# Attention, last two head pairs: values of both pairs in one PSUM bank, row sums in another, and exponentials of two key tiles added before they are summed

## The chip, the cores and the metric

The kernel runs on one core of a Trainium2 chip. The metric is the device time of one execution in microseconds (us). A core has five engines that each work through their own queue in order and wait for one another by semaphores: TensorE (PE in the profile; its weight loads are listed apart as PEld), VectorE (DVE), ScalarE (ACT), GpSimd (POOL) and SyncE (SP), which only issues DMAs here. TensorE writes its results into PSUM, which this kernel divides into eight banks of 128 partitions by 512 float32.

## The reference, cut to what matters

```python
x  = hidden_states                          # (1, 2048, 512), float32
xn = layernorm(x)
qkv = xn @ w_qkv.T                          # 16 heads of 32
scores = where(causal, (q @ k.T) / sqrt(32), lowest)
attn = softmax(scores) @ v                  # per head, 2048 x 2048 scores
out = x + attn @ w_o.T + ffn(xn)            # ffn: gated GELU, 512 -> 4096 -> 512, 4-bit weights
```

Softmax is computed as exp(score - row maximum), summed over the keys for each query ("row sums"), and the values' product is divided by that sum at the end.

## The kernel before, in words

Sixteen heads are handled as eight pairs (`NP = 8`). Queries go in four blocks of 512 columns (`qb` 0 to 3), keys in sixteen tiles of 128 (`kt`). Scores are made transposed: keys on the partitions, 512 queries along the columns. A *step* `n` is one key tile for one query block, `steps[n] = (qb, kt)`; there are 40 steps per pair. In a block, the last four key tiles (`kt >= 4 * qb`) are *diagonal*: only columns from `c0 = (kt - 4 * qb) * 128` on are computed, so their widths are 512, 384, 256 and 128. The other steps are *off-diagonal* and 512 wide. Block 0 has no off-diagonal steps, block 1 has 4, block 2 has 8 and block 3 has 12.

Pairs 0 to 5 run one at a time, each together with the search for the row maxima of a later pair. Their row sums are already taken from exponentials that GpSimd adds up over two steps (`add_up`, line 395) and that TensorE then sums with a matrix of ones (`add_rows`, line 354).

The last two pairs (6 and 7), for which no maxima remain to be found, run *together* in a loop over `together`, a list of the 40 steps in an order written out by hand: blocks in the order 1, 0, 2, 3, and in a block each diagonal step followed by a quarter of the off-diagonal ones. Nothing is rescheduled: the order in which the code calls the operations is the order of each engine's queue. One pass of this loop issues:

1. `score_cols` (line 280) and `add_scores` (line 295): for each of the four heads one small bf16 matmul that puts minus the row maximum into a PSUM bank, and one float32 matmul that adds the scores. Pair 6 uses the pool `ps_t`, pair 7 the pool `ps_s`, each of three banks, so a step's two banks of a pool are free again only when exponentials of the step before have been read out of them.
2. `attend` for the step before, called for pair 6 and then for pair 7: `add_values` (line 343), two matmuls of values with the exponentials of two heads, and `add_rows` (line 354), two of ones with the same exponentials. A pair's values lie in partitions 0 to 63 of one bank and its row sums in partitions 64 to 127 of the same bank (`m0` for pair 6, `m1` for pair 7).
3. The exponentials, pair 6 head 0, head 1, then pair 7 head 0, head 1. Off-diagonal steps only need ScalarE (line 309). A diagonal step first has VectorE limit the diagonal 128 columns to at most 0 in PSUM (line 643, "the limit"), then ScalarE's exponential (line 646), then GpSimd sets the keys that come after the query to 0 (`omit_later_keys`, line 324). They are written to `prob` tiles of [128, 2, 512], one for a pair and a step, from a pool of five.
4. What is left over: at a block's end `keep_attention` copies the two banks out (lines 422 and 423), `normalize_attention` then inverts the row sums in four parts on VectorE (line 444) and multiplies on GpSimd (line 446); and eight times `token_rest` prepares the tokens for the feed-forward part (line 656 on VectorE, "the mask"; line 659 on GpSimd; line 661 on VectorE in a later pass).

After the loop come the output projection (`po`, line 889, 64 matmuls), which TensorE begins with block 1, and the feed-forward part (lines 934 to 1009), which fills the rest of the span.

Of the kernel before, what the change touches and what calls it, by code (L numbers as in the profile page):

```python
# [38 lines left out]
F32 = mybir.dt.float32  # L39
F32R = mybir.dt.float32r  # L40
I32 = mybir.dt.int32
AF = mybir.ActivationFunctionType
ALU = mybir.AluOpType
# [3 lines left out]
P = 128  # L47
# [3 lines left out]
D = H // HEADS  # L51
NT = S // P
TB = 512
NTB = S // TB
NK = H // P
NOG = H // P
NP = HEADS // 2
# [17 lines left out]
STEPS = NTB * (NTB + 1) * 2  # L75
# [3 lines left out]
def block_kernel(  # L79
# [10 lines left out]
    nc = tc.nc  # L90
# [4 lines left out]
    def turn_tile(i, name, dtype=F32, shape=(P, TB)):  # L95
# [6 lines left out]
    aT = [  # L102
        [late.tile([P, TB], F32, tag=f"aT{og}_{b}", name=f"aT{og}_{b}") for b in range(NTB)]
        for og in range(NOG)
    ]
# [8 lines left out]
    with (  # L114
# [23 lines left out]
        ones = const.tile([P, D], F32, tag="ones", name="ones")  # L138
# [3 lines left out]
        v = [vals.tile([P, 4, H], F32, tag=f"v{b}", name=f"v{b}") for b in range(NTB)]  # L142
# [42 lines left out]
        units, steps, first = [], [], {}  # L185
# [80 lines left out]
        def rows_when_due():  # L266
            if due and tick[0] >= due[0][0]:
                rows_from_parts()
            tick[0] += 1
# [33 lines left out]
        def exponentials(p, n, tiles):  # L303
            qb, kt = steps[n]
            c0 = max(0, kt - 4 * qb) * P
            prob = probs.tile([P, 2, TB], F32, tag="prob", name=f"prob{p}_{n}")
            if kt < 4 * qb:
                for h, ps in enumerate(tiles):
                    nc.scalar.activation(prob[:, h, :], ps, AF.Exp)  # L309
                return prob  # L310


            clip = turn_tile(12 + n % 2, f"clip{p}_{n}", shape=(P, 2, P))
            for h, ps in enumerate(tiles):
                nc.scalar.activation(clip[:, h], ps[:, c0 : c0 + P], AF.Relu, scale=-1.0)
                if c0 + P < TB:
                    nc.scalar.activation(prob[:, h, c0 + P :], ps[:, c0 + P :], AF.Exp)
            diag = prob[:, :, c0 : c0 + P]
            nc.scalar.activation(diag, clip, AF.Exp, scale=-1.0)
            omit_later_keys(diag)  # L320
            return prob

        def omit_later_keys(diag):
            nc.gpsimd.affine_select(
                out=diag,
                in_=diag,
                compare_op=ALU.is_ge,
                fill=0.0,
                base=0,
                pattern=[[0, 2], [1, P]],  # L330
                channel_multiplier=-1,
            )

        avs, rows, sums = {}, {}, {}
# [64 lines left out]
        def attend(p, n, prob, first, last):  # L399

            qb, kt = steps[n]
            if first:
                avs[p, qb] = ps_m.tile([P, TB], F32, tag=f"m{p % 2}", name=f"av{p}_{qb}")
                rows[p, qb] = avs[p, qb]
            add_values(p, n, prob, 0, first, last)
            c0 = max(0, kt - 4 * qb) * P
            add_rows(p, qb, [prob[:, h] for h in range(2)], first, last, c0)
            if last:
                full.append((p, qb))

        full, invert = [], []

        def keep_attention():

            p, qb = full.pop(0)
            av, row = avs[p, qb], rows[p, qb]
            og, half = p // 2, slice(64 * (p % 2), 64 * (p % 2 + 1))
            if p % 2 == 0:
                sums[og, qb] = sump.tile([P, TB], F32, tag="sums", name=f"sums{og}_{qb}")
            if p >= NP - 2:  # L420
                copy = nc.vector.tensor_copy if p % 2 else nc.scalar.copy
                copy(aT[og][qb][half], av[:64])
                copy(sums[og, qb][half], row[64:])
            else:
                if qb == 0:
                    nc.scalar.copy(aT[og][qb][half], av[:64])
                else:
                    both = turn_tile(8 + p % 2, f"both{p}_{qb}")
                    nc.scalar.copy(both, av)  # L429
                nc.vector.tensor_copy(sums[og, qb][half], row[64:])  # L430
                if qb > 0:
                    other = slice(64 * (1 - p % 2), 64 * (2 - p % 2))
                    nc.scalar.copy(aT[og][qb][half], both[other])
                    nc.gpsimd.tensor_tensor(
                        aT[og][qb][half], aT[og][qb][half], both[half], ALU.add
                    )
            if p % 2 == 1:
                invert.extend((og, qb, i) for i in range(4))
# [95 lines left out]
        for b in range(NTB):  # L534
            n = first[b]
# [5 lines left out]
            for i in range(4):  # L541
# [5 lines left out]
                for j in range(b + 1):  # L547
                    rows_when_due()
                    tiles = [score_rows(0, n, ps_s), score_rows(1, n, ps_t)]
# [11 lines left out]
        todo, at, quads = {}, [0], 0  # L561

        def later_on(wait, f, *args):
            todo.setdefault(at[0] + wait, []).append((f, args))

        def run_due(m):
            for f, args in todo.pop(m, []):
                f(*args)

        for m in range((NP - 2) * STEPS):  # L570
            p, n = divmod(m, STEPS)
# [5 lines left out]
            ps = score_cols(p, n, ps_t)  # L577
# [3 lines left out]
            prob = exponentials(p, n, ps)  # L581
# [3 lines left out]
            qb, kt = steps[n]  # L585
# [6 lines left out]
            else:  # L592
                added = add_up(2 * quads + kt % 4 // 2, even, prob)
# [32 lines left out]
        together = []  # L626
        for qb in TOGETHER:
            mine = [n for n in range(STEPS) if steps[n][0] == qb]
            for d in range(4):
                together += [mine[4 * qb + d], *mine[d * qb : (d + 1) * qb]]  # L630

        def diagonal(n):
            return steps[n][1] >= 4 * steps[n][0]

        def exponentials_together(p, n, tiles):
            if not diagonal(n):
                return exponentials(p, n, tiles)
            qb, kt = steps[n]
            c0 = (kt - 4 * qb) * P
            prob = probs.tile([P, 2, TB], F32, tag="prob", name=f"prob{p}_{n}")  # L640
            for h, ps in enumerate(tiles):

                nc.vector.tensor_scalar(
                    ps[:, c0 : c0 + P], ps[:, c0 : c0 + P], 0.0, None, ALU.min
                )
                nc.scalar.activation(prob[:, h, c0:], ps[:, c0:], AF.Exp)
            omit_later_keys(prob[:, :, c0 : c0 + P])
            return prob

# [2 lines left out]
        def token_rest(b, k, high):  # L654
            xk, (low, mixed) = xnT[b][:, k], lm[b, k]
            nc.vector.tensor_scalar(
                high.bitcast(I32), xk.bitcast(I32), HIGH, None, ALU.bitwise_and
            )
            nc.gpsimd.tensor_tensor(low, xk, high, ALU.subtract)
            yield  # L660
            nc.vector.scalar_tensor_tensor(
                mixed, high, SPLIT, low.bitcast(F32), ALU.mult, ALU.subtract
            )
            yield

        pending = []
        early = [(i, k) for i in range(2) for k in range(NK)]
        rest = iter(())
        for s, n in enumerate(together):
            rows_when_due()  # L670
            two = [score_cols(NP - 2, n, ps_t), score_cols(NP - 1, n, ps_s)]
            for i in range(2):
                add_scores(NP - 2 + i, n, two[i])
            for m in sorted(todo):
                run_due(m)
            while pending:
                attend(*pending.pop(0))
            qb = steps[n][0]
            ends = [
                s == 0 or steps[together[s - 1]][0] != qb,  # L680
                s == STEPS - 1 or steps[together[s + 1]][0] != qb,
            ]
            for i in range(2):
                prob = exponentials_together(NP - 2 + i, n, two[i])
                pending.append((NP - 2 + i, n, prob, *ends))
            while full:
                keep_attention()
            if invert:
                normalize_attention()
            next(rest, None)  # L690
            if early and s % 2 == 0 and not diagonal(together[s + 1]):
                i, k = early.pop(0)
                b = ORDER[i]
                lm[b, k] = [
                    turn_tile(8 * i + 2 * k + part, f"lm{b}_{k}_{part}", F32R)
                    for part in range(2)
                ]
                rest = token_rest(b, k, qkp.tile([P, TB], F32, tag=f"qk{k % 2}", name=f"hx{b}_{k}"))
                next(rest)
        assert not early  # L700
        while pending:
            attend(*pending.pop(0))
        while full:
            keep_attention()
        while invert:
            normalize_attention()

# [374 lines left out]
```

## Time and profile before

| | |
|---|---|
| median of 3 runs | 1966.24 us (1964.48 to 1968.52) |
| the profiled execution, its own time | 1963.04 us |
| its span in the profile | 1961.3 us, granted TensorE clock 1.0 |
| TensorE matmul busy | 1925.9 us (98%) |
| VectorE, ScalarE, GpSimd busy | 1325.1, 1102.9, 928.0 us |
| loop of the last two pairs | first limit at 708.96 us, first exponential at 709.36 us, first `po` matmul at 826.12 us |
| output projection | 826.12 to 880.75 us |

Times in the timelines are counted from the start of the span. A row of a timeline gives the start, the time from the first instruction's start to the last one's end, the engine, the line of the kernel, the operation, what it writes and reads, and how many instructions were merged into the row. A float32 matmul appears as two records. Matmuls overlap one another: those of different row groups or column groups of the array run side by side, so the distance between starts tells more than the length of one.

### The profile page before, as it was taken

What the parts mean: (1) busy time and instruction counts of PE and PEld (TensorE: products, weight loads), DVE (VectorE), ACT (ScalarE), POOL (GpSimd) and SP (SyncE); (2) the same over time, 40 slices, a digit from 0 to 9 for tenths busy, and PEclk for the clock granted to TensorE, in tenths of its full rate; (3) what the DMA queues carried; (4) which work ended last, traced back from release to release, by engine and by line L of the source; (5) the groups of instructions that cost most, each with busy time, mean ns of one, the idle gap of its engine ahead of it and who ended that gap; (6) DMA issues with size and microseconds to landing.
All of it is one profiled execution on the core that took longest, in us unless ns stands there. A gap on an engine that the chain in (4) does not pass through costs nothing.

```text
span 1961.3 us, 32383 instructions
## 1 busy us (share of the span) xinstructions
PE 1925.9 (98%) x11648; PEld 1181.8 (60%) x11648; DVE 1325.1 (68%) x2706; ACT 1102.9 (56%) x2299; POOL 928.0 (47%) x1055
## 2 busy tenths in 40 slices
PE   7999999999999999999999999999999999999998
PEld 3433333333333332348888888888888888888886
DVE  5657675657556764187777777767677777777774
ACT  2112665556556666536666666666666666666664
POOL 1000655545545653155555564545555555556551
PEclk9999999999999999999999999999999999999999
DMA  3000000000000001110000000000000000000002
GB/s 129 1 12 11 2 2 1 2 12 2 2 1 12 2 2 36 29 56 22 20 21 21 18 24 19 22 19 22 19 20 20 22 20 21 21 21 22 18 5 86
DMA packets 55392, 39.86 MB, mean 20 GB/s; under 512 B 14784, under 2 KB 47552, under 8 KB 55232
## 3 DMA queue, kind: packets, MB, share of 16 engines
q1 hardware_dynamic: 55232, 37.81, 6.6%
q8 instruction: 91, 1.49, 0.3%
q14 instruction: 69, 0.57, 0.1%
HBM read 33.55 MB, written 4.19 MB: 19 GB/s over the span
## 4 chain that ended last, share of the span: by engine, by line
PE 94%; ACT 3%; POOL 1%; issue 1%; DVE 1%; DMA 0%; DVEq 0%; ACTq 0%; POOLq 0%
PE gu L934 24%; PE gu L947 12%; PE pd L997 12%; PE av L343 10%; PE ps_s L209 9%; PE pd L1009 6%; PE ps_qk L165 6%; PE ps_t L280 4%; PE ps_t L295 3%; PE ps_v L515 3%; PE po L889 3%; ACT prob L309 2%; POOL added L395 1%; PE ptx L504 0%; PE pm L261 0%
## 5 line engine op out<-in xcount | busy, mean ns | idle before, releaser
L934 PE MATMUL gu<-xh,gu 128*128 128x512 f32 x1024 | 403.9, 394 | 0.0
L934 PE MATMUL gu<-lm,gu 128*128 128x512 f32 x1024 | 403.7, 394 | 0.0
L233 DVE TENSOR_REDUCE tops<-ps_s 128x1 f32<-128x512 f32 x384 | 243.2, 680 | 155.9 <-PE ps_s L209 131.2
L1018 DVE SCALAR_TENSOR_TENSOR acc<-pd,acc 128x512 f32<-128x512 f32 x512 | 316.9, 680 | 2.4 <-PE pd L1009 2.4
L979 POOL TENSOR_TENSOR parts<-inter,hi 128x512 fp32r<-128x512 f32 x128 | 171.2, 1338 | 278.1 <-DVE hi L975 272.9
L209 PE MATMUL ps_s<-qk,qk 32*128 32x512 f32 (+3 forms) x1280 | 288.6, 576 | 0.0
L309 ACT ACTIVATE prob<-ps_t 128x512 f32<-128x512 f32 x384 | 205.9, 596 | 138.4 <-PE ps_t L295 121.5
L947 PE MATMUL gu<-lm,gu 128*128 128x512 f32 x1024 | 279.7, 395 | 0.0
L971 DVE SCALAR_TENSOR_TENSOR inter<-gu,gate 128x512 f32<-128x512 f32 x128 | 88.5, 692 | 275.4 <-PE gu L947 275.4
L295 PE MATMUL ps_t<-qk,qk 32*128 32x512 f32 (+3 forms) x1280 | 266.9, 537 | 0.0
L1004 ACT ACTIVATE pd<-pd 128x512 f32<-128x512 f32 x512 | 263.3, 581 | 1.1 <-PE pd L997 1.1
L343 PE MATMUL av<-prob,v 128*32 128x128 f32 (+3 forms) x1856 | 257.6, 425 | 5.5 <-ACT both L429 4.2
L997 PE MATMUL pd<-wd,parts 128*128 128x512 f32 x1024 | 259.6, 396 | 0.0
L941 ACT ACTIVATE gu<-gu 128x512 f32<-128x512 f32 x256 | 148.6, 581 | 188.3 <-PE gu L934 188.3
L395 POOL TENSOR_TENSOR added<-prob,prob 128x512 f32<-128x512 f32 x144 | 179.6, 1269 | 109.7 <-ACT prob L309 109.2
L947 PEld LDWEIGHTS gu<-lm,gu 128*128 128x128 f32 x1024 | 192.0, 188 | 47.1 <-issue 0.2
L934 PEld LDWEIGHTS gu<-lm,gu 128*128 128x128 f32 x1024 | 191.9, 187 | 46.6 <-POOL wd L804 0.2
L997 PEld LDWEIGHTS pd<-wd,parts 128*128 128x128 f32 x1024 | 192.3, 188 | 45.8
L934 PEld LDWEIGHTS gu<-xh,gu 128*128 128x128 f32 x1024 | 192.0, 188 | 45.7 <-ACT wd L803 0.2
L343 PEld LDWEIGHTS av<-prob,v 128*32 128x32 f32 x1856 | 67.2, 108 | 206.2 <-issue 148.3
L228 DVE CUSTOM_DVE_ANT_0 ps_s<-ps_s,mask_qk 128x128 f32<-128x128 f32 (+3 forms) x256 | 120.8, 517 | 88.8 <-PE ps_t L295 50.9
L978 ACT CAST parts<-hi 128x512 fp32r<-128x512 f32 x128 | 79.7, 623 | 172.7 <-DVE hi L975 171.0
(106 smaller groups left out, 2934.2 us busy)
## 6 DMA issues: line engine op xcount, KB each, us to landing
pk<-packed SPq DMA_DIRECT2D x96, 128.0 KB, 2.2
sc<-scales SPq DMA_DIRECT2D x512, 8.0 KB, 1.6
x<-x SPq DMA_DIRECT2D x16, 256.0 KB, 3.9
acc<-x SPq DMA_DIRECT2D x16, 256.0 KB, 3.0
sc<-scales SPq DMA_DIRECT2D x256, 16.0 KB, 1.7
out<-acc SPq DMA_DIRECT2D x16, 256.0 KB, 2.2
wqk<-w_qk SPq DMA_DIRECT2D x4, 512.0 KB, 4.2
wv<-w_v SPq DMA_DIRECT2D x4, 256.0 KB, 5.7
```

The costliest lines, as they stand in the source:

```text
L209: nc.tensor.matmul(ps[:, :w], lhsT=qT[p // 2, qb][rows, i * P : (i + 1) * P], rhs=kT[p // 2, c][rows, :w], start=True, stop=True,)
L233: nc.vector.tensor_reduce(top, ps[:, :w], AX.X, ALU.max)
L295: nc.tensor.matmul(ps[:, c0:], lhsT=kT[p // 2, kt // 4][rows, (kt % 4) * P : (kt % 4 + 1) * P], rhs=qT[p // 2, qb][rows, c0:], start=False ...
L309: nc.scalar.activation(prob[:, h, :], ps, AF.Exp)
L343: nc.tensor.matmul(avs[p, qb][D * j : D * (j + 1), c0:c1], lhsT=v[kt // 4][:, kt % 4, D * head : D * (head + 1)], rhs=prob[:, h, c0:c1], s ...
L395: nc.gpsimd.tensor_tensor(t, prob_a[:, h], prob_b[:, h], ALU.add)
L934: nc.tensor.matmul(ps, lhsT=parts[:, i, k], rhs=mov, start=(k == 0 and i == 0), stop=(k == NK - 1 and i == 1),)
L947: nc.tensor.matmul(ps, lhsT=gu[g, m, j][:, 2, k], rhs=lm[b, k][1], start=False, stop=(k == NK - 1), skip_group_check=True,)
L979: nc.gpsimd.tensor_tensor(parts[:, 1], inter, high, ALU.subtract)
L997: nc.tensor.matmul(po, lhsT=parts[:, part, i * P : (i + 1) * P], rhs=w[:, part], start=(part == 0), stop=(part == 1),)
L1004: nc.scalar.activation(po, po, AF.Copy, scale=HIGH_SCALE)
L1018: nc.vector.scalar_tensor_tensor(acc[t], po, SUM_SCALE, acc[t], ALU.mult, ALU.add)
```

## The change

The loop of the last two pairs is rewritten.

- The values of all four heads go into one bank (`m0`, 32 partitions a head) and the row sums of all four into another (`m1`): `values_together` and `rows_together`, four matmuls each.
- In an off-diagonal couple (an even and the following odd key tile) the exponentials of both steps are first added, pair 6 by GpSimd and pair 7 by VectorE, two adds of [128, 512] on each, and the row sums are taken from the four sums, two steps after the odd one. Diagonal steps still give their row sums directly, one step later (two for a block's first step).
- The exponentials of a step come in the order head 0 of pair 6, head 0 of pair 7, head 1 of pair 6, head 1 of pair 7.
- The order of steps in a block is in whole couples: in block 1 diagonal, diagonal, two off-diagonal, twice; in block 3 chunks of 2, 4, 2 and 4.
- Values and row sums are copied out in one instruction each, 128 partitions wide. The eight sums and one place for the mask lie in buffers of the pool `qk`. `token_rest` starts in every fourth pass.

```diff
             for d in range(4):
-                together += [mine[4 * qb + d], *mine[d * qb : (d + 1) * qb]]
+                c0, c1 = (qb * e // 2 * 2 for e in (d, d + 1))
+                together += [mine[4 * qb + d], *mine[c0:c1]]
...
+        def exponentials_together(n, two):
...
+            for h in range(2):
+                for i in range(2):
+                    ps = two[i][h]
+                    if diagonal(n):
+                        diag = ps[:, c0 : c0 + P]
+                        nc.vector.tensor_scalar(diag, diag, 0.0, None, ALU.min)
+                    nc.scalar.activation(both[i][:, h, c0:], ps[:, c0:], AF.Exp)
+            if diagonal(n):
+                for i in range(2):
+                    omit_later_keys(both[i][:, :, c0 : c0 + P])
+            return both
+
+        def values_together(n, both, first, last):
...
+            for j in range(4):
+                head = 2 * (NP - 2) + j
+                nc.tensor.matmul(
+                    avs[NP, qb][D * j : D * (j + 1), c0:],
+                    lhsT=v[kt // 4][:, kt % 4, D * head : D * (head + 1)],
+                    rhs=both[j // 2][:, j % 2, c0:],
+                    start=first, stop=last,
+                )
...
+        def rows_together(qb, exps, c0, first, last):
...
+            for j in range(4):
+                nc.tensor.matmul(
+                    rows[NP, qb][D * j : D * (j + 1), c0:],
+                    lhsT=ones, rhs=exps[j][:, c0:], start=first, stop=last,
+                )
...
+        added = [
+            qkp.tile([P, TB], F32, tag=f"qk{j % 2}", name=f"added_last{j}") for j in range(8)
+        ]
...
-            for m in sorted(todo):
-                run_due(m)
-            while pending:
-                attend(*pending.pop(0))
...
-            for i in range(2):
-                prob = exponentials_together(NP - 2 + i, n, two[i])
-                pending.append((NP - 2 + i, n, prob, *ends))
+            run_due(s)
+            both = exponentials_together(n, two)
...
+            later_on(1, values_together, n, both, first, last)
+            if diagonal(n):
+                exps = [both[j // 2][:, j % 2] for j in range(4)]
+                c0 = (kt - 4 * qb) * P
+                later_on(2 if first else 1, rows_together, qb, exps, c0, first, last)
+            elif kt % 2 == 0:
+                before = both
+            else:
+                place = added[4 * (couples % 2) : 4 * (couples % 2) + 4]
+                couples += 1
+                for j in range(4):
+                    add = (nc.gpsimd, nc.vector)[j // 2].tensor_tensor
+                    add(place[j], before[j // 2][:, j % 2], both[j // 2][:, j % 2], ALU.add)
+                later_on(2, rows_together, qb, place, 0, False, last)
             if invert:
                 normalize_attention()
             next(rest, None)
-            if early and s % 2 == 0 and not diagonal(together[s + 1]):
+            if early and s % 4 == 3:
...
-                rest = token_rest(b, k, qkp.tile([P, TB], F32, tag=f"qk{k % 2}", name=f"hx{b}_{k}"))
+                rest = token_rest(b, k, high_place)
                 next(rest)
```

More of the change, by code (lines that the diff above doesn't have):

```diff
@@ L629, in block_kernel @@
             for d in range(4):
-                together += [mine[4 * qb + d], *mine[d * qb : (d + 1) * qb]]
+                c0, c1 = (qb * e // 2 * 2 for e in (d, d + 1))
+                together += [mine[4 * qb + d], *mine[c0:c1]]
         def diagonal(n):
             return steps[n][1] >= 4 * steps[n][0]
-        def exponentials_together(p, n, tiles):
-            if not diagonal(n):
-                return exponentials(p, n, tiles)
+        def exponentials_together(n, two):
             qb, kt = steps[n]
[L639 to L644, printed above, removed]
-                )
-                nc.scalar.activation(prob[:, h, c0:], ps[:, c0:], AF.Exp)
-            omit_later_keys(prob[:, :, c0 : c0 + P])
-            return prob
+            c0 = max(0, kt - 4 * qb) * P
+            both = [
+                probs.tile([P, 2, TB], F32, tag="prob", name=f"prob{NP - 2 + i}_{n}")
+                for i in range(2)
+            ]
[10 more added lines that the diff above has]
+            return both
@@ new lines, in values_together @@
+        def values_together(n, both, first, last):
+            qb, kt = steps[n]
+            c0 = max(0, kt - 4 * qb) * P
+            if first:
+                avs[NP, qb] = ps_m.tile([P, TB], F32, tag="m0", name=f"av_last{qb}")
+            for j in range(4):
[4 more added lines that the diff above has]
+                    rhs=both[j // 2][:, j % 2, c0:],
+                    start=first,
+                    stop=last,
+                )
+            if last:
+                kept.append(("values", qb))
@@ new lines, in rows_together @@
+        def rows_together(qb, exps, c0, first, last):
+            if first:
+                rows[NP, qb] = ps_m.tile([P, TB], F32, tag="m1", name=f"rows_last{qb}")
+            for j in range(4):
+                nc.tensor.matmul(
+                    rows[NP, qb][D * j : D * (j + 1), c0:],
+                    lhsT=ones,
+                    rhs=exps[j][:, c0:],
+                    start=first,
+                    stop=last,
+                )
+            if last:
+                kept.append(("rows", qb))
@@ new lines, in block_kernel, with keep_together @@
+        kept = []
+        def keep_together():
+            what, qb = kept.pop(0)
+            if what == "values":
+                nc.scalar.copy(aT[NOG - 1][qb], avs[NP, qb])
+            else:
+                sums[NOG - 1, qb] = sump.tile([P, TB], F32, tag="sums", name=f"sums_last{qb}")
+                nc.vector.tensor_copy(sums[NOG - 1, qb], rows[NP, qb])
+                invert.extend((NOG - 1, qb, i) for i in range(4))
+        added = [
+            qkp.tile([P, TB], F32, tag=f"qk{j % 2}", name=f"added_last{j}") for j in range(8)
+        ]
@@ L652, in block_kernel @@
+        high_place = qkp.tile([P, TB], F32, tag="qk1", name="high_place")
         lm = {}
@@ L664, in token_rest @@
             yield
-        pending = []
         early = [(i, k) for i in range(2) for k in range(NK)]
-        rest = iter(())
+        rest, couples = iter(()), 0
+        last_n = {steps[n][0]: n for n in together}
         for s, n in enumerate(together):
+            at[0] = s
             rows_when_due()
@@ L673, in block_kernel @@
                 add_scores(NP - 2 + i, n, two[i])
-            for m in sorted(todo):
-                run_due(m)
-            while pending:
-                attend(*pending.pop(0))
[L678 to L682, printed above, removed]
-            for i in range(2):
-                prob = exponentials_together(NP - 2 + i, n, two[i])
-                pending.append((NP - 2 + i, n, prob, *ends))
+            if s == 0:
+                for m in sorted(todo):
+                    run_due(m)
+            run_due(s)
+            qb, kt = steps[n]
+            both = exponentials_together(n, two)
             while full:
                 keep_attention()
+            while kept:
+                keep_together()
+            first = s == 0 or steps[together[s - 1]][0] != qb
+            last = n == last_n[qb]
+            later_on(1, values_together, n, both, first, last)
[5 more added lines that the diff above has]
+                before = both
+            else:
+                place = added[4 * (couples % 2) : 4 * (couples % 2) + 4]
[4 more added lines that the diff above has]
+                later_on(2, rows_together, qb, place, 0, False, last)
             if invert:
@@ L697, in block_kernel @@
                 ]
-                rest = token_rest(b, k, qkp.tile([P, TB], F32, tag=f"qk{k % 2}", name=f"hx{b}_{k}"))
+                rest = token_rest(b, k, high_place)
                 next(rest)
         assert not early
[L701 to L704, printed above, removed]
+        next(rest, None)
+        for m in sorted(todo):
+            run_due(m)
+        while kept:
+            keep_together()
         while invert:
```

## The prediction

> **What bounds the kernel now.** I first read the page, to see which engine the span hangs on, then the loop's own timeline. The page alone would say TensorE:
>
> ```profile
> span 1961.3 us, 32383 instructions
> PE 1925.9 (98%) x11648; PEld 1181.8 (60%) x11648; DVE 1325.1 (68%) x2706; ACT 1102.9 (56%) x2299; POOL 928.0 (47%) x1055
> PE 94%; ACT 3%; POOL 1%; issue 1%; DVE 1%; DMA 0%; DVEq 0%; ACTq 0%; POOLq 0%
> L395 POOL TENSOR_TENSOR added<-prob,prob 128x512 f32<-128x512 f32 x144 | 179.6, 1269 | 109.7 <-ACT prob L309 109.2
> ```
>
> But 98% is an average, and only the loop from 709.36 us (first exponential) to 826.12 us (first `po` matmul), 116.8 us, is changed. Its timeline, one part of block 2 (a diagonal step 128 wide, two off-diagonal steps, the next diagonal step), ScalarE with some rows of VectorE and TensorE:
>
> ```profile
> 766.76 2.06 ACT L309 ACTIVATE prob<-ps_t 128x512 f32<-128x512 f32 x4 [0.78 <-PE ps_t L295]
> 769.17 0.89 DVE L643 TENSOR_SCALAR ps_t<-ps_t 128x128 f32<-128x128 f32 x4 [3.89 <-PE ps_t L295]
> 769.56 0.84 ACT L646 ACTIVATE prob<-ps_t 128x128 f32<-128x128 f32 x4 [0.73 <-DVE ps_t L643]
> 772.20 2.06 ACT L309 ACTIVATE prob<-ps_t 128x512 f32<-128x512 f32 x4 [1.80 <-PE ps_t L295]
> 773.83 0.37 PE L280 MATMUL ps_t<-neg,ones_h 3*128 3x512 bf16 x1 [0.59 <-ACT prob L309]
> 773.83 1.23 PE L295 MATMUL ps_t<-qk,qk 32*128 32x512 f32 x8
> 775.05 2.06 ACT L309 ACTIVATE prob<-ps_t 128x512 f32<-128x512 f32 x4 [0.78 <-PE ps_t L295]
> 778.59 1.57 ACT L646 ACTIVATE prob<-ps_t 128x512 f32<-128x512 f32 x3 [1.48 <-DVE ps_t L643]
> ```
>
> TensorE and ScalarE hold each other. At 773.83 TensorE's fourth small matmul waits until the third exponential (1.57 after 772.20) has emptied its bank, and the next exponential follows 1.22 later. VectorE's limits stand in this ring too: ScalarE cannot begin a diagonal step before them, and here VectorE waits for TensorE, 3.89 us idle. Whatever is put ahead of the limits in VectorE's queue lengthens the ring.
>
> A full TensorE step, and a row from an earlier stage:
>
> ```profile
> 810.03 0.40 PE L280 MATMUL ps_t<-neg,ones_h 3*128 3x512 bf16 x4
> 810.26 1.03 PE L295 MATMUL ps_t<-qk,qk 32*128 32x512 f32 x8
> 811.22 0.62 PE L343 MATMUL av<-prob,v 128*32 128x512 f32 x2
> 813.08 0.23 PE L280 MATMUL ps_t<-neg,ones_h 3*128 3x128 bf16 x4
> 505.62 0.85 PE L343 MATMUL av<-prob,v 128*32 128x384 f32 x8
> ```
>
> Scores take 1.19, values and row sums 1.86: two groups (one a pair) of 0.86 and 0.13 for switching. The last row is values from two `prob` tiles at once, four different moving operands: eight records in 0.85. So four heads' values run side by side as two heads' values and row sums do.
>
> **The change, part by part.** *Removed:* each off-diagonal step's two groups (1.72) become values (0.86) and, once a couple, row sums (0.86): 0.43 saved in 24 steps, 10.3 us of TensorE. Diagonal steps keep two groups. *Moved:* in the new order of exponentials the fourth small matmul waits for the second exponential, 0.49 earlier. *Added:* per couple two GpSimd adds and two VectorE adds, all with both inputs in SBUF. Line 395 prices GpSimd's at 1.27; for VectorE the nearest row is line 861, 0.68. They wait for the odd step's exponentials, and behind VectorE's adds stand the limits of the next diagonal step. Can the two engines add at once? The output projection's timeline has such neighbours:
>
> ```profile
> 843.76 1.27 POOL L804 TENSOR_TENSOR gu<-w,high 128x512 fp32r<-128x512 f32 x1
> 844.19 1.39 DVE L661 SCALAR_TENSOR_TENSOR lm<-highx,lm 128x512 fp32r<-128x512 f32 x1
> 845.11 1.60 POOL L805 TENSOR_TENSOR gu<-gu 128x512 fp32r<-128x512 f32 x1
> L861 DVE TENSOR_TENSOR xh<-xnT,lm x8: 676/680/840, 846.9 to 868.8; 128x512 fp32r<-128x512 f32 x8
> ```
>
> No. Line 661, 0.69 when alone, began at 844.19 while GpSimd ran, and ended 0.55 after GpSimd's end (845.03). GpSimd's next, begun at 845.11, ended at 846.71, 1.13 after VectorE's 845.58. They take turns, 0.55 and 1.13, their starts of about 0.14 being the only overlap.
>
> [...]
>
> From the odd step's first exponential (time 0; exponentials end at 0.60, 1.09, 1.57, 2.06): GpSimd's first add 0.70 to 1.97; VectorE's first, ready at 1.19, ends 2.52; GpSimd's second 3.65; VectorE's second 4.20; the limit 0.29 and 0.10 to ScalarE: 4.59. Now by intervals between first exponentials:
>
> - *Odd step to diagonal step, 9 times* (before, 2.6 to 3.5; 3.54 in the rows above): 4.59 and what else the new program has between second add and limit: reciprocal and mask twice, reciprocal twice, mask twice, line 661 once, nothing twice. With 0.94, 0.42 and 0.69 that is 6.1 in all: 47.4.
> - *Diagonal to off-diagonal, 10 times* (before 2.3 to 3.1): end of the second exponential plus 1.22, by width 2.31, 2.10, 1.88, 1.69: 19.8.
> - *Even to odd behind a diagonal step, 10 times:* TensorE does the last couple's row sums 0.86, the diagonal's values and row sums (0.65, 0.43 or 0.22 each), 0.13, scores and start 1.35: 3.64, 3.20 or 2.77 (before 2.85 to 3.3); with 3.2 behind a block's first and 2.3 where no couple is due, 31.6.
> - *In block 3's chunks of four, odd to the next odd, twice:* of five `prob` tiles the second exponential of the even step needs one that GpSimd reads until 3.65; plus 0.60 and 1.22: 5.47, together 10.9 (two such steps took about 6.0 before).
> - *Diagonal to diagonal, 6 times:* the ten-fold class plus 0.39 for the limit gives 14.6, by the old ones (first exponentials at 732.07, 736.58, 739.02, 740.92 and 743.20, a mean of 2.78) it is 16.7; I take the middle, 15.6.
> - *Last odd step to `po`:* rows wait for VectorE's 4.20, then 0.1, 0.86, 0.1: 5.2 (before 3.4).
>
> Sum 130.5 against 116.8: +13.7. The 10.3 us of TensorE are real but fall into waits.
>
> At nothing go: the wider copies (one 0.58 on ScalarE and one 0.69 on VectorE for two of each, at four block ends), `token_rest` every fourth pass (the eight preparations are needed in the projection, 826 on), GpSimd's omitted keys (0.41, twice a diagonal step as before). SyncE: loads of `acc`, then the first weight words, now wait for buffers that the last row sums read, so the first scales are issued a few us after `po` begins, not at 821.61; their first reader ran at 837.8, 11.7 after `po` began, and the decoded weights are needed only at 880.75. Without that cover each us late would cost a us. The rest of the span only shifts.
>
> **The rivals.**
> *TensorE sets the pace:* the 10.3 us come off, 1956. The page's 98% and 94% speak for it. The wait at 773.83 speaks against. It decides if the nine intervals from odd step to diagonal step stay near 2.6; the balance turns at 5.27 - 13.7 / 9 = 3.75.
> *Adds side by side:* VectorE's second add ends at 2.06 + 0.10 + 0.68 = 2.84 instead of 4.20, 1.36 less nine times, and about 1.5 at the end and in the chunks of four: 1966 to 1968, not to be told from no change but for 0.01. The timelines of lines 661 and 805 speak against.
> *Longer turns:* if GpSimd's two adds go first, VectorE ends at 1.97 + 1.27 + 0.55 + 0.69 = 4.48, 0.28 more nine times, 1982.5; with the omitted keys also in turn (0.52 to 0.61 instead of 0.41 beside VectorE's mask in the trace), up to 0.2 in each of 16 steps, 1986.
> *Four values in a row instead of side by side* would cost 28 us and more; the row at 505.62 excludes it.
>
> **The numbers.** The profiled execution took 1963.04 (span 1961.3 and 1.7 around it); with 13.7 it is 1976.7. The median of the runs, 1966.24, lies 3.2 higher: 1980. Chances: turns as computed or somewhat longer, up to 1985, 0.74; longer still 0.07; side by side 0.12; TensorE's pace 0.07. From 1967 to 1985 leaves the last and part of two others out. A measurement of this kernel tells about 0.2%, 3.9 us, from no change: faster 0.07, same 0.11, slower 0.82.
>
> **What would show it.** In the changed profile: VectorE's adds at 1.3 to 1.7 instead of 0.68, GpSimd's second at 1.6; ScalarE's exponentials of diagonal steps idle 2 us or more before VectorE's limit; TensorE's values and row sums in the loop down by 10.3 us with more idle time than was saved; `po` at about 840. VectorE's adds at 0.68 would prove the turns wrong, and intervals from odd to diagonal step under 3.75 the sign.

## The result, and the profile after

The changed kernel took 1986.76 us (median of 5 runs, 1982.51 to 1989.39) against 1966.24: a ratio of 1.0097 with a 95% interval of 1.0084 to 1.0110. It is slower, as predicted, but 6.8 us slower than the 1980.0 foretold, and 1.8 us beyond the upper end of the range.

The page, of the execution that took 1986.76 us itself:

```profile
span 1985.0 us, 32221 instructions
PE 1935.6 (98%) x11552; PEld 1183.7 (60%) x11552; DVE 1357.0 (68%) x2726; ACT 1100.4 (55%) x2295; POOL 963.3 (49%) x1079
PEclk9999999999999999899999999999999999999999
```

TensorE runs 96 instructions fewer and yet is 9.7 us longer busy; the third row, the granted clock in 40 slices, has an 8 in it. Where the time went is read from three marks. The first exponential of the loop stands at 712.90 us (before 709.36), the first `po` matmul at 849.82 (826.12), the first `gu` matmul at 904.46 (880.75). So 3.5 us lie ahead of the loop, 20.1 in it (136.9 against 116.8), and nothing behind it (54.6 both). The 3.5 us are not the change's: in code that is the same, this execution had half its clock for 6.83 us from 193.6 us on, while the execution before had its whole clock over the same microseconds:

```profile
190.20:193.60 3.40, 1.67 (x16) 1.00 0.35 136
193.60:200.40 6.80, 6.49 (x35) 0.50 0.00 0
```

Such a row gives a stretch and its length, then TensorE's busy time with the number of its records, the granted clock, and two columns of DMA.

The loop by busy time of each engine and granted clock, first before, then after:

```profile
709.40:826.10 116.70, 110.82 (x1132) 34.47 (x1124) 45.14 (x106) 77.46 (x170) 32.60 (x64) 1.00 0.06 17
```
```profile
712.90:849.80 136.90, 116.87 (x1036) 35.35 (x1028) 77.21 (x127) 77.50 (x168) 68.36 (x88) 0.94 0.02 5
```

Here the busy times of PE, PEld, DVE, ACT and POOL come after the length, then the clock and DMA. ScalarE does the same work. VectorE and GpSimd are 32 and 36 us longer busy, though their 48 adds cost only 0.69 and 1.27 each when alone, 47 us in all. TensorE has 96 records fewer (12 groups of 0.86, the 10.3 us) and gained idle time instead: 20.0 us against 5.9. And the clock was 0.94 on average.

A couple's adds and the diagonal step behind them, from the timeline of the loop after:

```profile
721.74 2.06 ACT L652 ACTIVATE prob<-ps_t 128x512 f32<-128x512 f32 x4 [0.90 <-PE ps_t L295]
722.41 2.95 POOL L755 TENSOR_TENSOR added_last<-prob,prob 128x512 f32<-128x512 f32 x2 [3.43 <-ACT prob L652]
722.86 3.06 DVE L755 TENSOR_TENSOR added_last<-prob,prob 128x512 f32<-128x512 f32 x2 [4.67 <-ACT prob L652]
725.84 0.94 DVE L444 RECIPROCAL sums<-sums 128x128 f32<-128x128 f32 x1
726.70 0.36 DVE L712 TENSOR_SCALAR high_place<-xnT 128x512 int32<-128x512 int32 x1
726.98 0.87 DVE L651 TENSOR_SCALAR ps_t<-ps_t 128x128 f32<-128x128 f32 x4
727.78 0.49 PE L280 MATMUL ps_t<-neg,ones_h 3*128 3x128 bf16 x3 [2.54 <-ACT prob L652]
```

The adds end 3.62 (GpSimd) and 4.18 us (VectorE) after the odd step's first exponential; 3.65 and 4.20 were forecast. The limits (line 651) begin behind them, a reciprocal and a mask; the exponentials follow at 727.35, 5.61 after those of the odd step; and TensorE's small matmuls have waited 2.54 us. The waits over the whole loop, TensorE's and ScalarE's, before and after:

```profile
PE ps_t L280 <- ACT prob L309: 3.1, 6, 0.6
PE ps_t L280 <- ACT prob L646: 1.4, 3, 0.6
...
ACT prob L646 <- DVE ps_t L643: 15.6, 16, 1.5
```
```profile
PE ps_t L280 <- ACT prob L652: 18.3, 13, 2.6
...
ACT prob L652 <- DVE ps_t L651: 25.2, 13, 3.0
```

Columns: time in all, times, longest. ScalarE waits 3.0 us at most for a limit where it waited 1.5, and TensorE waits for the exponentials 18.3 us where it waited 4.5 (3.1 and 1.4). That is the ring as foretold. What was not foretold is what TensorE's waits do to its clock. Three pairs of neighbouring stretches, cut at the clock's own steps (each half-clock record in the loop is 3.41 us long), TensorE's busy time and granted clock alone:

```profile
739.80:743.20 3.40, 0.82 (x10) 0.99 0.00 0
743.20:746.60 3.40, 3.40 (x24) 0.50 0.00 0
780.70:784.10 3.40, 1.90 (x13) 1.00 0.02 5
784.10:787.50 3.40, 2.98 (x39) 1.00 0.00 0
...
821.70:825.10 3.40, 2.04 (x20) 1.00 0.00 0
825.10:828.50 3.40, 3.40 (x24) 0.50 0.01 2
```

After a stretch in which TensorE was busy for 0.82 to 2.04 of 3.40 us, it ran the next 3.41 us at half its clock (a half-clock window), five times in the loop (the others at 729.5, 794.4 and 808.0, behind 1.67, 1.62 and 1.67 us). The stretches at 780.7, with 1.90 us, and at 831.9, with 2.08 us, were not followed by one.

### The profile page after: what moved, and what is told of

Same layout as the page of the kernel before. It is cut to its first block, busy times and chain, and to the rows that moved or that the text cites. A ratio compares the mean times of both kernels' runs of the same rounds, so it can differ in the third digit from the quotient of the medians.

```text
span 1985.0 us, 32221 instructions
## 1 busy us (share of the span) xinstructions
PE 1935.6 (98%) x11552; PEld 1183.7 (60%) x11552; DVE 1357.0 (68%) x2726; ACT 1100.4 (55%) x2295; POOL 963.3 (49%) x1079
## 4 chain that ended last, share of the span: by engine, by line
PE 91%; ACT 4%; DVE 2%; POOL 2%; issue 1%; DMA 0%; DVEq 0%; ACTq 0%; POOLq 0%
PE gu L1004 24%; PE gu L1017 12%; PE pd L1067 12%; PE ps_s L209 9%; PE av L343 7%; PE ps_qk L165 6%; PE pd L1079 6%; PE ps_t L280 4%; PE ps_v L515 3%; PE po L959 3%; PE ps_t L295 3%; ACT prob L309 2%; PE rows_last L680 1%; DVE added_last L755 1%; POOL added L395 1%
## 5 line engine op out<-in xcount | busy, mean ns | idle before, releaser
L295 PE MATMUL ps_t<-qk,qk 32*128 32x512 f32 (+3 forms) x1280 | 272.2, 547 | 0.0
L309 ACT ACTIVATE prob<-ps_t 128x512 f32<-128x512 f32 x288 | 156.2, 594 | 116.2 <-PE ps_t L295 99.3
L343 PE MATMUL av<-prob,v 128*32 128x128 f32 (+3 forms) x1536 | 192.3, 404 | 4.2 <-ACT both L429 4.2
L848 POOL TENSOR_TENSOR w<-mag,sc 128x256 f32<-128x256 f16 x128 | 92.7, 745 | 162.6 <-DVE mag L836 159.3
```

Of the source, the lines that this page charges most:

```text
L295: nc.tensor.matmul(ps[:, c0:], lhsT=kT[p // 2, kt // 4][rows, (kt % 4) * P : (kt % 4 + 1) * P], rhs=qT[p // 2, qb][rows, c0:], start=False ...
L343: nc.tensor.matmul(avs[p, qb][D * j : D * (j + 1), c0:c1], lhsT=v[kt // 4][:, kt % 4, D * head : D * (head + 1)], rhs=prob[:, h, c0:c1], s ...
```

## The experiments

**First: the adds taken apart.** The theory: turns of VectorE and GpSimd make the limits late. The rival: the new layout (banks, order of steps) costs it. Only GpSimd's adds left out, only VectorE's left out, all four on VectorE, all four on GpSimd, and none, with all row sums taken directly. Where one engine's adds are left out, the row sums of its pair lack the even steps' exponentials; the other three kernels compute everything.

```diff
 # GpSimd's adds left out
-                for j in range(4):
...
+                place = [both[0][:, 0], both[0][:, 1], *place[2:]]
+                for j in range(2, 4):
+                    nc.vector.tensor_tensor(
...
 # VectorE's adds left out
-                for j in range(4):
...
+                place = [*place[:2], both[1][:, 0], both[1][:, 1]]
+                for j in range(2):
+                    nc.gpsimd.tensor_tensor(
...
 # all on VectorE (all on GpSimd: nc.gpsimd in the last line)
-                for j in range(4):
-                    add = (nc.gpsimd, nc.vector)[j // 2].tensor_tensor
+                for j in (0, 2, 1, 3):
+                    add = nc.vector.tensor_tensor
 # no adds, rows direct
-            elif kt % 2 == 0:
-                before = both
             else:
...
+                exps = [both[j // 2][:, j % 2] for j in range(4)]
+                later_on(1, rows_together, qb, exps, 0, False, last)
```

> GpSimd's adds are left out: pair 6's row sums take the odd step's exponentials alone (the even step's are missing from them); all else is the changed kernel. Theory 'turns' (VectorE's and GpSimd's adds exclude each other and hold up the limits behind them): VectorE's adds fall from about 1.5 us to 0.68, the nine intervals from odd step to diagonal step from a mean of 5.1 to about 3.9, the loop (first exponential to first po matmul) from 136.9 to about 117, and with fewer waits TensorE's clock stays at 1.0: near 1966 us. Rival 'layout' (the new banks, order of steps and copies cost the time, the adds run side by side): VectorE's adds keep their length, the loop stays above 130, about 1985 us.

> VectorE's adds are left out: pair 7's row sums take the odd step's exponentials alone; GpSimd's stay. Turns: GpSimd's adds at 1.27 both, nothing of the adds ahead of the limits, the odd to diagonal intervals near 2.6 to 3.5 again, the loop about 111, 1959 to 1962 us, below the kernel before since TensorE keeps its 10.3 us of saved row sums. Layout: about 1985 us as before. A third view, that GpSimd's adds themselves hold the prob buffers and so the time: still above 130 in the loop.

> All four adds of a couple on VectorE, none on GpSimd; the result is complete. Turns: four adds of 0.68 that start with the first exponential, the last ending 0.70 + 4 * 0.68 = 3.4 after it, limit at 3.8 instead of 4.6: odd to diagonal about 4.4 with what else is queued, the loop about 123 to 125 (some clock halving left), 1971 to 1975 us: better than the changed kernel though VectorE does twice the adds. Rival (VectorE's own queue is the trouble, not the turns): twice the work on it is worse, over 1990 us. Layout: 1985 us.

> All four adds of a couple on GpSimd, none on VectorE; the result is complete. No turns, and nothing of the adds ahead of the limits; but GpSimd needs 4 * 1.27 = 5.1 us a couple and holds four of five prob buffers until then, and its omitted keys of the next diagonal step stand behind the adds. Turns: odd to diagonal intervals back to about 3, yet diagonal to off-diagonal ones over 4 (ScalarE waits for buffers, values for omitted keys): the loop about 133, 1980 to 1987 us. Rival (only the sharing between the two engines costs): near 1960 us.

> No adds at all: each off-diagonal step gives its own row sums, as the diagonal ones do, one step later; banks, order of exponentials, order of steps and copies as in the changed kernel; the result is complete. Turns: TensorE's 10.3 us come back, but the loop is about 114, a little under the 116.8 of before because the fourth small matmul waits for the second exponential: 1963 to 1965 us. Layout: the loss stays, about 1985 us.

Measured, with the loop (first exponential to first `po`), the sum of its nine intervals from odd to diagonal step, and the number of half-clock windows in it, each from the profiled execution:

| | median us | ratio to before, 95% | loop us | nine intervals us | half-clock windows |
|---|---|---|---|---|---|
| changed kernel | 1986.76 | 1.0097 (1.0084 to 1.0110) | 136.9 | 45.5 | 5 |
| GpSimd's adds left out | 1965.84 | 0.9995 (0.9985 to 1.0004) | 114.3 | 34.1 | 0 |
| VectorE's adds left out | 1957.49 | 0.9956 (0.9942 to 0.9970) | 109.4 | 24.2 | 0 |
| all adds on VectorE | 1969.54 | 1.0017 (1.0008 to 1.0027) | 122.1 | 36.9 | 3 |
| all adds on GpSimd | 1978.34 | 1.0059 (1.0045 to 1.0073) | 132.9 | 24.2 | 3 |
| no adds, rows direct | 1961.64 | 0.9980 (0.9970 to 0.9989) | 113.7 | 29.8 | 0 |

The layout is cleared: with it and without the adds the kernel is slightly faster than before. The adds' lengths (smallest, median, largest in ns), VectorE's and GpSimd's each alone, then both in the changed kernel:

```profile
L755 DVE TENSOR_TENSOR added_last<-prob,prob x24: 691/693/694, 719.5 to 821.9; 128x512 f32<-128x512 f32 x24
```
```profile
L755 POOL TENSOR_TENSOR added_last<-prob,prob x24: 1266/1272/1282, 722.9 to 820.5; 128x512 f32<-128x512 f32 x24
```
```profile
L755 POOL TENSOR_TENSOR added_last<-prob,prob x24: 1267/1372/1727, 722.4 to 846.5; 128x512 f32<-128x512 f32 x24
L755 DVE TENSOR_TENSOR added_last<-prob,prob x24: 864/1478/1761, 722.9 to 847.0; 128x512 f32<-128x512 f32 x24
```

Either engine's adds are of one length when the other leaves them alone, and VectorE's double beside GpSimd's. GpSimd's alone delay no limit (24.2). All on GpSimd leaves the nine intervals short as well, and is slow by another way: the omitted keys of a diagonal step stand behind 5.1 us of adds in GpSimd's queue, and the `prob` buffers come free late. ScalarE's wait for these adds in that kernel:

```profile
ACT prob L652 <- POOL added_last L755: 16.3, 13, 2.2
```

Four of the five came out 1.4 to 1.7 us under the lower ends of their forecasts. With all adds on GpSimd, the intervals from diagonal to off-diagonal step took 3.2 us on average, where over 4 was expected.

**Second: what the saving is worth.** All four adds left out, the row sums taken once a couple from the odd step's exponentials only:

```diff
-                for j in range(4):
-                    add = (nc.gpsimd, nc.vector)[j // 2].tensor_tensor
-                    add(place[j], before[j // 2][:, j % 2], both[j // 2][:, j % 2], ALU.add)
+                place = [both[j // 2][:, j % 2] for j in range(4)]
```

> All four adds are left out: TensorE takes the row sums once a couple from the odd step's exponentials (the even steps' are left out of the row sums), so TensorE saves its 10.3 us and nothing else changes. The loop took 113.7 us with all row sums taken directly and 109.4 us with GpSimd's two adds alone. If the ring of limits, exponentials and small matmuls sets the pace, the 10.3 us come off only in part and GpSimd's adds lie beside it: a loop of 107 to 109.5, 1955 to 1959. If TensorE sets the pace, all of it comes off: a loop of 103.5, 1951 to 1953, and GpSimd's adds alone cost 6.

Measured: 1956.79 us, ratio 0.9953 (0.9936 to 0.9970), a loop of 107.0. Of TensorE's 10.3 us, 6.7 come off (113.7 to 107.0) when nothing is to be paid for them. GpSimd's two adds a couple cost 2.4 of that (109.4), VectorE's two 7.3 (114.3). Both together, if they only added up, would give 116.7, an estimate that equals the loop before (116.8): even without turns the adds would have eaten all that the change saves. A complete kernel with GpSimd's adds alone, pair 7's row sums taken directly, was not run.

**Third: the new order of exponentials alone,** in the kernel before:

```diff
+            for h in range(2):
+                for i in range(2):
...
+                    nc.scalar.activation(both[i][:, h, c0:], ps[:, c0:], AF.Exp)
             for i in range(2):
-                prob = exponentials_together(NP - 2 + i, n, two[i])
...
```

> The kernel before with one thing of the change alone: the exponentials in the order head 0 of pair 6, head 0 of pair 7, head 1 of pair 6, head 1 of pair 7. The fourth small matmul then waits for the second exponential instead of the third (0.49 earlier). Reckoned from the ring in the trace: the steps that ScalarE bounds get up to 0.49 shorter, the full ones of 3.04 not: the loop about 113 instead of 116.8, 1962 to 1964 us, faster than both kernels. Rival: TensorE's own 3.04 a step decides everywhere, no change, 1966 us.

Measured: 1962.95 us, ratio 0.9981 (0.9972 to 0.9990), loop 113.1. This one edit brings what the whole layout without adds brings (113.7): one bank for all values, another for all row sums and the order in couples add nothing measurable to it in the loop. These two kernels, which compute everything, beat the kernel before by 0.2% and the changed one by 1.2 to 1.3%; nothing run here that computes everything was faster.

**Fourth: the clock.** The theory: some 7 of the missing us are not waits but work done at half clock after them. TensorE is given extra small matmuls, into a bank that is overwritten at once, while it waits for the nine diagonal steps behind a couple; they fill TensorE's waits, change no other engine's work and bring no limit forward. Eight, and then four:

```diff
+            fill = s >= 2 and diagonal(together[s - 1]) and not diagonal(together[s - 2])
-            two = [score_cols(NP - 2, n, ps_t), score_cols(NP - 1, n, ps_s)]
+            two = [score_cols(NP - 2, n, ps_t, 8 * fill), score_cols(NP - 1, n, ps_s)]
...
+                for _ in range(fill * (1 - h)):
+                    nc.tensor.matmul(
+                        ps, lhsT=ones_h, rhs=negs[p // 2, 0], start=True, stop=True
+                    )
```

> The changed kernel, and eight extra small matmuls (bf16, 512 columns, about 0.21 us each) into a bank that is overwritten right after, ahead of the first small matmul of each step behind a diagonal step that follows an off-diagonal one: TensorE waits there for 2 to 3 us for the limits. Theory 'clock' (in the changed kernel the granted clock was 0.5 in five windows of 3.4 us of the loop, each behind a stretch in which TensorE streamed for less than about 0.6 of the time; this costs about 7 us beyond the 13.7 forecast): the extra work keeps the clock at 1.0 in the loop and the time falls by about 5 to 7 us, to 1980 or so, although TensorE does 72 matmuls more. Rival (the half clock is only a sign, the waits cost the time themselves): no change, 1986, or up to 15 us slower if the extra matmuls are not hidden.

> Four extra small matmuls (about 0.85 us) in each of the nine waiting steps instead of eight. TensorE was busy 21% to 59% of the 3.4 us before each half-clock window; 0.85 us more lifts that by a quarter. If the clock goes by the busy share of such a stretch (about half needed), 0 to 2 half-clock windows are left: 1978 to 1982. If it goes by the longest idle stretch, which 0.85 us hardly shortens, 4 or 5 are left: 1985 to 1988.

| | median us | ratio to before, 95% | loop us | nine intervals us | half-clock windows |
|---|---|---|---|---|---|
| no extra matmuls | 1986.76 | 1.0097 (1.0084 to 1.0110) | 136.9 | 45.5 | 5 |
| four | 1981.84 | 1.0076 (1.0061 to 1.0091) | 132.0 | 45.6 | 2 |
| eight | 1978.49 | 1.0059 (1.0045 to 1.0072) | 129.0 | 45.5 | 0 |

Work was added and the kernel became 8.3 us faster. The nine intervals, in which the waits lie, did not move by 0.1; only the half-clock windows went, at 1.5 to 1.6 us of loop each. TensorE over the same place of the loop, without extra matmuls and with eight (line 281):

```profile
742.23 0.34 PE L280 MATMUL ps_t<-neg,ones_h 3*128 3x384 bf16 x2 [2.64 <-ACT prob L652]
...
744.00 1.94 PE L680 MATMUL rows_last<-added_last,ones 128*32 128x512 f32 x8
```
```profile
737.53 1.90 PE L281 MATMUL ps_t<-neg,ones_h 128*128 128x512 bf16 x8
...
740.49 0.34 PE L284 MATMUL ps_t<-neg,ones_h 3*128 3x384 bf16 x2 [0.80 <-ACT prob L656]
...
741.88 1.06 PE L684 MATMUL rows_last<-added_last,ones 128*32 128x512 f32 x8
```

The wait of 2.64 us is followed by a group of row sums that takes 1.94 us instead of 1.06. With four extra matmuls the two half-clock windows that are left again follow the stretches in which TensorE was least busy; 1.79 us and, at 739.2, 1.58; one with 2.50 us was not followed by one:

```profile
725.50:728.90 3.40, 1.79 (x22) 1.00 0.00 0
728.90:732.30 3.40, 3.40 (x28) 0.50 0.00 0
...
763.10:766.50 3.40, 2.50 (x23) 1.00 0.02 5
766.50:769.90 3.40, 3.40 (x40) 1.00 0.00 0
```

**Fifth: the same adds behind the limits.** If the queue is what makes the turns dear, adds that stand behind the next step's limits should cost little. The exponentials must then be kept longer, so pair 7's go to the buffers of the sums, and the sums overwrite the even step's exponentials; once as in the change, once with all four adds on VectorE:

```diff
             both = exponentials_together(n, two)
+            add_waiting()
...
-                for j in range(4):
-                    add = (nc.gpsimd, nc.vector)[j // 2].tensor_tensor
-                    add(place[j], before[j // 2][:, j % 2], both[j // 2][:, j % 2], ALU.add)
-                later_on(2, rows_together, qb, place, 0, False, last)
+                waiting.append((before, both, qb, last))
```

> The same adds of the same two engines, but each couple's four adds are queued behind the limits of the step that follows, and the exponentials are kept longer for it (pair 7's lie in the buffers that held the sums; the sums overwrite the even step's). If the time is lost because the limits stand behind adds that take turns, the nine intervals from odd to diagonal step fall from 45.5 us to what they are without VectorE's adds or without any (24.2 to 29.8), no half-clock window is left in the loop, and the time is 1958 to 1968. If the turns themselves are the cost, wherever the adds stand in the queue, the intervals only move the loss to other steps: 1975 or more.

> As the kernel with the adds behind the limits, with all four adds of a couple on VectorE. No turns are left, and no add stands before a limit: 1956 to 1966 by the theory of the queue. If VectorE's 48 adds of 0.69 are too much for it wherever they stand, as in the kernel with all adds on VectorE before the limits: 1969 or more.

Measured: 1968.54 us with both engines (ratio 1.0006, 0.9997 to 1.0016), 1967.21 with VectorE alone (1.0001, 0.9991 to 1.0010); loops of 118.7 and 118.6, nine intervals of 30.2 and 27.8, no half-clock window in either loop. Moving the adds takes back 18 of the 20 us, the clock's 7.9 among them. It does not show that the place in the queue alone made the turns dear, for most turns went too: VectorE's adds had a median of 0.68 us there instead of 1.48, and its busy time in the loop fell from 77.2 to 62.3 us. With all adds on VectorE hardly any turns are left in either place (adds of at most 0.69 and 0.89 us), and moving them took the nine intervals from 36.9 to 27.8 us, but the loop only from 122.1 to 118.6, which the three half-clock windows that went (4.5 to 4.8 us by estimate, at 1.5 to 1.6 each) would account for alone. Both measured times lie just over the forecast's upper ends, 1968 and 1966: the loop is still 5 us longer than without adds, so the saving stays lost. It is spread over other steps. VectorE and GpSimd now wait for TensorE before some adds (6.9 and 3.8 us, twice each), since the sum overwrites what the values still read, and the six intervals from diagonal to diagonal step took 19.5 and 21.0 us, against 16.3 without adds. The edit also sets pair 7's omitted keys to 0 in two instructions a diagonal step instead of one (medians of 0.29 us each with both engines and 0.73 with VectorE alone, against one of 0.41), which may be part of it. This remainder was not taken apart further.

## Why the prediction was right on the sign and wrong on the size

The forecast's classes of intervals beside what the profiles show, in us. The kernel with eight extra matmuls is the changed one with its clock whole in the loop.

| step of the prediction | forecast | clock whole | changed kernel |
|---|---|---|---|
| odd to diagonal, 9 times | 47.4 | 45.5 | 45.5 |
| diagonal to off-diagonal, 10 times | 19.8 | 21.0 | 23.5 |
| even to odd behind a diagonal, 10 times | 31.6 | 30.7 | 34.6 |
| odd to next odd in chunks of four, twice | 10.9 | 10.9 | 10.9 |
| diagonal to diagonal, 6 times | 15.6 | 15.5 | 17.2 |
| last odd step to `po` | 5.2 | 5.2 | 5.2 |
| loop | 130.5 | 129.0 | 136.9 |

**Right: the turns, and the ring.** 0.55 and 1.13 us as the turns' lengths, read off two neighbours in another stage, gave the adds' ends to 0.03 us (VectorE's second add ended at 4.17 or 4.18 in all twelve couples). That VectorE and GpSimd hold each other up is shown by the runs with one engine's adds: VectorE's took 0.69 us there and 1.48 (median) beside GpSimd's, GpSimd's 1.27 there and up to 1.73 beside VectorE's. The signs named came as named: VectorE's adds of 1.4 to 1.8 where 1.3 to 1.7 was expected (0.86 where GpSimd had begun long before), GpSimd's second at 1.5 to 1.7. Where they stand, the turns cost 12.3 us more than each engine's adds alone do together (129.0 against 116.7).

**Right: TensorE does not set the pace.** The nine intervals of 5.06 on average lie far above the 3.75 named as the point where the sign turns. The 10.3 us were real work but could not all be had: 6.7 with no adds at all.

**Right: nothing behind the loop.** The stretch from `po` to `gu` is 54.6 us in both. That `po` began at 849.8 and not at about 840 is the 3.5 us ahead of the loop and the term that follows.

**Wrong: a term is missing.** The sentence that failed is "the 10.3 us of TensorE are real but fall into waits": the prediction priced these waits as time in which TensorE stands still and loses nothing else. It had 1.00 as the granted clock of the whole loop before, and carried that over to a loop in which TensorE waits for exponentials 13 times, up to 2.64 us at a time. The five half-clock windows are worth 136.9 - 129.0 = 7.9 us; the intervals themselves were forecast 1.5 too long. The difference, 6.4, is nearly all of the 6.8 by which the forecast fell short; the rest is what the 3.5 us lost at 193.6 us exceed the 3.2 that the prediction added for the runs' median. The range's upper end, 1985, covered longer turns only. No rival held the clock either.

**Was it to be seen before?** Not as a number. The profile before has its clock at 0.50 only in its last 1.2 us (from 1960.1 us on), behind 3.4 us without a single matmul, and in its loop TensorE waited for exponentials 0.6 us at most. The stretches that came before the half-clock windows here had 0.82 to 2.04 of 3.40 us of TensorE work. From that profile the term could have been suspected, not counted.

The half clock at 193.6 us follows the same pattern, and it lets one kernel's runs differ. Six of the thirteen profiles have it, for two of the clock's steps each time, behind a step in which TensorE was busy for 1.7 to 2.0 us. In the other seven, if the clock's steps are counted back from the next clock change on record, the same dip is cut otherwise, TensorE was busy for 2.1 us or more in each step, and the clock stayed whole. Of the five runs of the changed kernel, two at a mean clock of 0.996 took 1982.51 us and stand inside the range; the others, at 0.993 and 0.992, took 1986.76 to 1989.39. The 3.5 us of the stretch at 193.6 us could make most of the 4.3 us between 1982.51 and the median, and so could fewer half-clock windows in the loop. Which run lost what was not shown; only one was profiled.

## What to carry to other kernels

Work taken from the busiest engine helps only as far as the ring around it lets go (here 6.7 of 10.3 us, with no adds to pay for); before handing work to VectorE and GpSimd, look for what stands behind it in their queues (here limits, for which ScalarE then waited up to 3.0 us instead of 1.5), and price adds of both with their inputs in SBUF as turns, not side by side: here VectorE's took 1.48 us (median) beside GpSimd's and 0.69 alone. Where a change makes TensorE wait again and again (here 18.3 us in 13 waits, up to 2.64 us long), add a term for its clock: in these profiles every stretch of 3.4 us with up to 1.88 us of busy time was followed by a half-clock one, at 1.5 to 1.6 us each in the loop. The cheapest edit here, the order of four exponentials, was worth 3.6 us of the loop; no version with adds that computes everything was faster than the kernel before.

## What the runs showed of the hardware that was not expected

- Half-clock windows of 3.41 us follow stretches of the same length in which TensorE was busy, by the profile, for about half of the time, with no wait in the changed kernel's loop longer than 2.64 us. Over all thirteen profiles, leaving out their first and last microseconds, each of the 13 such stretches at whole clock with up to 1.88 us busy was followed by one and none with more than 2.20; in between, 6 of 17 were. So in these profiles the bound lies between 1.88 and 2.20 us of busy time (55 to 65% of a stretch), and can't be told closer from them.
- Useless matmuls in these waits make the kernel faster: 72 of them (1.90 us for eight) saved 8.3 us, 36 saved 4.9.
- VectorE's adds took 0.69 us alone and 1.48 (median) beside GpSimd's, GpSimd's 1.27 alone and up to 1.73 beside VectorE's.
